# End of a fused attention and feed-forward kernel: last attention output kept in SBUF, last pair of token tiles taken one by one, the closing list chosen from many orders

## Chip, cores and metric

The kernel runs on one NeuronCore of a Trainium2 chip. The metric is the device time of one execution in microseconds (us), here the median of three runs. The engines are TensorE (PE in the profile, its weight loads PEld), VectorE (DVE), ScalarE (ACT), GpSimd (POOL) and SyncE (SP), which issues all DMAs of this kernel.

## Reference

```python
x = x + tanh(g_xattn) * attention(layernorm(x), ctx)      # 16 heads of 32, pad mask over x's rows
x = x + tanh(g_ffn) * ffn(layernorm(x))
# attention: q = x Wq^T, k and v from ctx Wkv^T, softmax(q k^T / sqrt(32)) v
# ffn:  h = bitlinear(x, w1, b1); h = gelu(h) (exact); bitlinear(h, w2, b2)
# bitlinear: rmsnorm, activations rounded to 127 steps of the row's maximum,
#            weights rounded to -1, 0, 1 times their mean size
```

x is 32 x 224 x 512, ctx 32 x 750 x 384, w1 goes from 512 to 2048 and w2 back. All inputs are float32.

## Kernel before

**Tiling.** Attention is cut into 128 steps (b, g): 32 batches times 4 groups of 4 heads. A step has six slots `k`: the maxima of the scores (`sm`, DVE's `mx`), the weights (`se` on PE, then Exp into `p` on ScalarE, sums `acc` on GpSimd) and, for the step before, the values (`po`) and their sums. VectorE transposes `po` into `oT` and takes the reciprocal `rd` of the sums (`sums`); `finish` multiplies the two into `yo` on GpSimd; `store` writes `yo` with four DMAs (one per head) to `o_d`, a scratch tensor in DRAM that holds the attention output token by token.

The feed-forward part works on 56 tiles of 128 tokens, taken in 28 pairs (`TG = 2`, `NF = 28`, numbered 0 to 27). `ffn_units(i)` gives the units of one pair. For both tiles together: `load` (x; and `og`, the attention output, out of `o_d`), `add`, `stats`, `rsqrt`, `norm`, `max`, `sa0` to `sa2` (scales of the rounding), `grid`, `bias`, `round`, `turn` (two transposing DMAs into `xT`). For each tile t: `b{t}0` to `b{t}3` (PE's `ph` from `xT` and w1; VectorE writes h out of it), `gelu`, `square`, `hm` (maxima), `sb0` to `sb2` (scales), `cgrid`, `cround`, `cturn` (a transposing DMA into `hT`), `c{t}0` and `c{t}1` (PE's `po` from `hT` and w2; VectorE adds it to x), `out` (store). In the records the h of pair 26 is called `wq_sb` and `wkv_sb`, and x and attention output of the last two pairs are both `xo`, after the buffers that they reuse.

**Order.** Every instruction is kept in program order on its engine by a helper (line 52 of the kernel before, so nearly every record has that line). In the loop, `Ffn.fill` starts feed-forward units slot by slot where there is room and `ready` says that what they need was started long enough ago. A Gelu in the loop loads its table and then, by a dummy Exp called `warm`, the table of Exp again.

After the loop, `Ffn.drain` writes out everything that is left, one unit after the other: the last attention step (`top`: the copy of the negative maxima `nT`; `w0` to `w2`: weights; `val`, `fin0`, `sto0`: values, division and store of the step before; `vlast`, `fin1`, `sto1`: of the last step) and the rest of pairs 25, 26 and 27. It is one greedy list: of the units that could begin soonest, by planned durations `TAKES_US` and free times of the engines, the one with the longest way to the end goes next. For a unit with two ways (VectorE or GpSimd, ScalarE or VectorE) the planner chooses the earlier end, with VectorE's time counted twice; `small[0]` then holds the engine for the unit. `behind` lists what a unit has to stand behind; the fetch of the last pair's attention output stands behind `sto1`:

```python
"fetch": [(NF, "sto1")],
...
f"b{t}0": [(pair, "turn")]
```

Of the kernel before, what the change touches and what calls it, by code (L numbers as in the profile page):

```python
# [19 lines left out]
EPS = 1e-5  # L20
# [4 lines left out]
def flamingo_gated_layer(  # L25
# [420 lines left out]
    def finish(b, g):  # L446
# [6 lines left out]
        yo_of[b, g] = yo  # L453

    def store(b, g):
        yo = yo_of.pop((b, g))
        for j in range(HG):
            cols = slice(g * P + j * DH, g * P + (j + 1) * DH)
            sp.dma_start(
                o_d[b * S : (b + 1) * S, cols].rearrange("(c r) d -> r c d", r=DH),  # L460
                yo[j * DH : (j + 1) * DH],
            )
# [72 lines left out]


    draining = []
    NTI = NT // P
    TG = 2
    NF = NTI // TG  # L540

    def quant_scales(s, r, amax, n, tag, unit):

        a = smf.tile([P, n], F32, tag=f"{tag}_am", name=f"{tag}_am")
        c = smf.tile([P, n], F32, tag=f"{tag}_c", name=f"{tag}_c")
        s[tag] = c, a
        if n == 1:  # L550
            small[0].tensor_scalar(a, amax, r, 1e-5, ALU.mult, ALU.max)
        else:
            small[0].tensor_tensor(a, r, amax, ALU.mult)
            small[0].tensor_scalar(a, a, 1e-5, None, ALU.max)
        yield
        dve.reciprocal(c, a)
        yield
        if n == 1:
            small[0].tensor_scalar(c, c, 127.0, r, ALU.mult, ALU.mult)
        else:  # L560
            small[0].tensor_scalar(c, c, 127.0, None, ALU.mult)
            small[0].tensor_tensor(c, c, r, ALU.mult)
        small[0].tensor_scalar(a, a, unit, None, ALU.mult)
# [7 lines left out]
    def ffn_units(i):  # L571
# [6 lines left out]
        def a_load():  # L578
# [11 lines left out]
            if i < NF - 1:  # L590
                a_fetch()

        def a_fetch():
            sp.dma_start(s["og"], o_d[rows, :].rearrange("(t p) d -> p t d", p=P))

# [19 lines left out]
        def a_norm():  # L615
            if i < NF - 2:
                s["xc"] = fp.tile([P, TG, D], F32, tag="xc", name=f"xc_{i}")
            else:
                both = vp.tile([P, NKC * D // 2], F32, tag="v", name=f"xc_{i}")
                s["xc"] = both[:, : TG * D].rearrange("p (t d) -> p t d", t=TG)  # L620
                s["xq"] = both[:, TG * D :].bitcast(BF16).rearrange("p (t d) -> p t d", t=TG)
            for t in range(TG):
                to, of, by = s["xc"][:, t, :], s["xg"][:, t, :], s["nm"][:, t : t + 1]
                if small[0] is dve:
                    dve.tensor_scalar(to, of, by, None, ALU.add)
                else:
                    act.activation(to, of, AF.Identity, bias=by)
# [36 lines left out]
        def b_matmul(t, f):  # L664
# [11 lines left out]
            for k in range(NDC):  # L676
# [4 lines left out]
            dve.scalar_tensor_tensor(  # L681
                s["h", t][:, cols], ph, s["qa"][1][:, t : t + 1], b1_sb[:, cols],
                ALU.mult, ALU.add,
# [63 lines left out]
        ]  # L747
        if i == NF - 1:
            first[1:] = [("fetch", 0, "load", 0, 0, 0, a_fetch), ("add", 0, "fetch", 0, 0, 0, a_add)]
        first += [  # L750
# [10 lines left out]
            ("turn", 0, "round", 0, 0, 0, a_turn),  # L761
        ]
        parts = [first]
        for t in range(TG):
            part = []
            for f in range(4):
                part.append((
                    f"b{t}{f}", 0 if f else 3, f"b{t}{f - 1}" if f else "turn", 0.9, 0, 0.75,
                    lambda t=t, f=f: b_matmul(t, f),
                ))  # L770
# [32 lines left out]
        "sb2": [[("DVE", 0.4)], [("POOL", 0.6)]], "cgrid": [[("DVE", 1.7)], [("POOL", 2.0)]],  # L803
        "cround": [[("ACT", 2.0)], [("DVE", 1.8)]], "cturn": [[("SP", 3.8)]],
        "c": [[("PE", 1.75), ("DVE", 0.5)]], "out": [[("SP", 2.0)]],
        "top": [[("PE", 0.3), ("ACT", 0.4)]],
        "w": [[("PE", 1.1), ("ACT", 1.7)]],
        "val": [[("PE", 2.9), ("DVE", 0.9)]], "vlast": [[("PE", 4.0), ("DVE", 0.9)]],
        "fin": [[("POOL", 0.6)]], "sto": [[("SP", 3.6)]],
    }  # L810

    QUEUE_US = {"sto": 1.9, "turn": 1.9, "cturn": 1.5, "load": 0.5, "fetch": 0.5, "out": 0.4}

# [3 lines left out]
        for name, after in {  # L817
            "w0": "top", "w1": "w0", "w2": "w1", "val": "", "fin0": "val", "sto0": "fin0",
            "vlast": "w2 val", "fin1": "vlast fin0", "sto1": "fin1 sto0",
        }.items()  # L820
    }

    class Ffn:
# [3 lines left out]
        def __init__(self):  # L827
            self.slot = 0
            self.parts = []
            self.next = 0  # L830
            self.at = {}

        def behind(self, pair, name):
# [3 lines left out]
                "load": [(pair - XG, f"out{TG - 1}"), (pair - 1, "add")],  # L837
                "fetch": [(NF, "sto1")],
                "norm": [(pair - 1, "round")],
# [5 lines left out]
            if name[-1].isdigit():  # L845
                t = int(name[len(name.rstrip("0123456789"))])
                (p1, t1), (ph, th) = (divmod(pair * TG + t - n, TG) for n in (1, HB))
                before = {
                    f"b{t}0": [(pair, "turn")]
                    + [(ph - (pair == NF - 1), f"cround{th}")] * (pair != NF - 2),  # L850
# [12 lines left out]
        def ready(self, pair, unit):  # L863
            name, lag, after = unit[:3]
            lag = lag if not draining else 0
            if after is not None:
# [43 lines left out]
        def drain(self, more):  # L910
# [3 lines left out]
            draining.append(True)  # L914
            free = {"PE": 0.0, "ACT": 0.0, "DVE": 4.3, "POOL": 5.0, "SP": 0.0}
            end = {}

            def takes(name):
                kind = name.rstrip("0123456789")
                return TAKES_US.get(kind) or TAKES_US[kind + name[-1]]  # L920

            self.parts.insert(0, [NF, more])
            while self.next < NF:
                self.parts += [[self.next, part] for part in ffn_units(self.next)]
                self.next += 1
            left = {}

            def rank(at):

                if at not in left:  # L930
                    left[at] = 0.0
                    left[at] = sum(us for _, us in takes(at[1])[0]) + max(
                        (rank(x) for x in behind if at in behind[x]), default=0.0
                    )
                return left[at]

            behind = {
                (pair, u[0]): [(pair, u[2] or "")] + self.behind(pair, u[0])
                for pair, units in self.parts for u in units
            }  # L940

            def course(at, way):

                t = max(
                    [end.get(x, 0.0) for x in behind[at]
                     if x[1].rstrip("0123456789") not in ORDER_ONLY or x[1][:-1] != at[1][:-1]],
                    default=0.0,
                )
                t = begin = max(t, free[way[0][0]])
                for engine, us in way:  # L950
                    t = max(t, free[engine]) + us
                return begin, t

            while self.parts:
                self.slot += 10
                found = []
                for part in self.parts:
                    for unit in part[1]:
                        if self.ready(part[0], unit):
                            at = part[0], unit[0]  # L960
                            way = min(
                                takes(unit[0]), key=lambda way: course(at, way)[1]
                                + 1.0 * sum(us for engine, us in way if engine == "DVE"),
                            )
                            found.append((course(at, way)[0], -rank(at), part, unit, way))
                soon = min(f[0] for f in found) + 2
                t, _, part, unit, way = min((f for f in found if f[0] <= soon), key=lambda f: f[1])
                part[1].remove(unit)
                self.at[part[0], unit[0]] = self.slot
                small[0] = {"DVE": dve, "POOL": gp}.get(way[-1][0], act)  # L970
                unit[6]()
                for engine, us in way:
                    t = max(t, free[engine])
                    free[engine] = t + (QUEUE_US[unit[0].rstrip("0123456789")] if engine == "SP" else us)
                    t += us
                end[part[0], unit[0]] = t
                self.parts = [p for p in self.parts if p[1]]
            return end

# [52 lines left out]
    for n in range(N - 1):  # L1032
# [56 lines left out]
        for k in range(6):  # L1089
# [13 lines left out]
            if wunits:  # L1103
                if k in (1, 3, 5):
                    wunits.pop(0)()
            else:
                some = ffn.fill(
                    (PE_ROOM[k % 2] - used, (1.1, 2.2)[k % 2], 1.7),
# [18 lines left out]
            for name, at, *do in (  # L1127
                ("val", last[0], values, sums), ("fin0", last[0], finish), ("sto0", last[0], store),
                ("vlast", last[1], values, sums), ("fin1", last[1], finish), ("sto1", last[1], store),
            )  # L1130
# [40 lines left out]
```

## Time and profile before

| | us |
|---|---|
| median of three runs | 2996.57 (2995.82, 2996.57, 2997.93) |
| profiled execution, its own time | 2990.66 |
| its span | 2988.9 |
| PE busy | 2891.5 (97%) |
| POOL busy | 2081.6 (70%) |
| DVE busy | 1725.5 (58%) |
| ACT busy | 1417.8 (47%) |
| last 99 us (from 2890): PE busy | 59.5 |

The profile is of one execution. Its records tell when an instruction started on its engine, how long it took, and what ended an idle time ahead of it. The clock of PE is granted by a throttle, and the windows of the profile give its mean in parts of full speed. The median of the runs is 5.91 us above the profiled execution.

### The profile page before, as it was taken

What the parts mean: (1) busy time and instruction counts of PE and PEld (TensorE: products, weight loads), DVE (VectorE), ACT (ScalarE), POOL (GpSimd) and SP (SyncE); (2) the same over time, 40 slices, a digit from 0 to 9 for tenths busy, and PEclk for the clock granted to TensorE, in tenths of its full rate; (3) what the DMA queues carried; (4) which work ended last, traced back from release to release, by engine and by line L of the source; (5) the groups of instructions that cost most, each with busy time, mean ns of one, the idle gap of its engine ahead of it and who ended that gap; (6) DMA issues with size and microseconds to landing.
All of it is one profiled execution on the core that took longest, in us unless ns stands there. A gap on an engine that the chain in (4) does not pass through costs nothing.

```text
span 2988.9 us, 62964 instructions
## 1 busy us (share of the span) xinstructions
PE 2891.5 (97%) x26814; PEld 1839.9 (62%) x26814; DVE 1725.5 (58%) x2588; ACT 1417.8 (47%) x1438; POOL 2081.6 (70%) x2727
## 2 busy tenths in 40 slices
PE   8999999999999999999999999999999999999976
PEld 5666566666666666666666666666666666666643
DVE  5576555655555565556555555654655655556545
ACT  2344454544545455445445454553543554545444
POOL 3566767767777777767667777767767777687674
PEclk9999999999999999999999999999999999999987
DMA  5433223123222212221222222223122222321213
GB/s 152 106 95 98 54 57 79 35 59 73 53 58 63 58 48 70 65 68 32 57 72 53 58 61 64 46 58 75 44 49 65 48 69 63 69 74 27 46 45 79
DMA packets 376697, 190.03 MB, mean 64 GB/s; under 512 B 283104, under 2 KB 340576, under 8 KB 376288
## 3 DMA queue, kind: packets, MB, share of 16 engines
q1 hardware_dynamic: 376416, 186.02, 25.8%
q8 instruction: 209, 3.42, 0.5%
q14 instruction: 72, 0.59, 0.1%
HBM read 119.86 MB, written 29.39 MB: 50 GB/s over the span
## 4 chain that ended last, share of the span: by engine, by line
PE 82%; ACT 10%; POOL 3%; DVE 3%; issue 1%; DMA 1%; POOLq 0%; ACTq 0%; SPq 0%; DVEq 0%
PE po L52 17%; PE pk L52 14%; PE se L52 14%; PE sm L52 12%; PE pv_None L52 8%; ACT p L52 7%; PE ph L52 6%; PE pv L52 6%; PE pq L52 3%; DVE mx L52 2%; ACT L52 2%; POOL acc L52 1%; ACT h L52 1%; PE pn L52 1%; POOL r_a L52 1%
## 5 line engine op out<-in xcount | busy, mean ns | idle before, releaser
L52 POOL TENSOR_TENSOR acc<-acc,p 125x896 f32<-125x896 f32 x510 | 1066.0, 2090 | 325.7 <-ACT p L52 304.2
L52 DVE TENSOR_REDUCE mx<-sm 112x4 f32<-112x2000 f32 (+1 forms) x384 | 861.0, 2242 | 664.5 <-PE sm L52 662.6
L52 ACT ACTIVATE p<-se 125x1792 f32<-125x1792 f32 x384 | 639.1, 1664 | 759.0 <-PE se L52 701.6
L52 PE MATMUL pk<-y,wkv_sb 128*128 128x375 f32 x1536 | 538.3, 486 | 2.0 <-DMA y<-in_ctxT 2.0
L52 PE MATMUL sm<-kT,qT 32*112 32x500 f32 (+1 forms) x4096 | 426.7, 508 | 31.6 <-ACT p L52 22.7
L52 POOL TENSOR_TENSOR acc<-p 125x896 f32<-125x896 f32 x128 | 268.3, 2096 | 244.4 <-ACT p L52 244.3
L52 PEld LDWEIGHTS pk<-y,wkv_sb 128*128 128x128 f32 x1536 | 277.8, 189 | 174.4 <-issue 34.5
L52 PE MATMUL se<-qT,kT 32*125 32x224 f32 x6144 | 359.5, 348 | 0.0
L52 PE MATMUL po<-p,v 125*32 125x224 f32 x6144 | 318.1, 355 | 0.0
L52 PE MATMUL pv<-wkv_sb,y 128*125 128x256 f32 x1248 | 311.0, 385 | 0.0
L52 PEld LDWEIGHTS se<-qT,kT 32*125 32x125 f32 x6144 | 295.5, 183 | 0.0
L52 PEld LDWEIGHTS sm<-kT,qT 32*112 32x112 f32 x4096 | 159.2, 170 | 190.1 <-ACT p L52 138.7
L52 PEld LDWEIGHTS po<-p,v 125*32 125x32 f32 x6144 | 186.9, 110 | 119.5 <-issue 44.0
L52 PEld LDWEIGHTS pv<-wkv_sb,y 128*125 128x125 f32 x1248 | 223.2, 188 | 52.3 <-issue 17.8
L52 ACT COPY kT<-pk 128x375 f32<-128x375 f32 x256 | 120.3, 470 | 278.8 <-PE pk L52 278.0
L52 PE MATMUL pv_None<-wkv_sb,y 128*125 128x256 f32 x1056 | 250.9, 387 | 0.0
L52 PEld LDWEIGHTS pv_None<-wkv_sb,y 128*125 128x125 f32 x1056 | 191.2, 187 | 89.0 <-issue 59.7
L52 PE MATMUL po<-w2q,hT 128*128 128x256 fp8e4 x1792 | 222.1, 280 | 24.4 <-DMA hT<-hq 24.4
L52 DVE SCALAR_TENSOR_TENSOR h<-ph,qa_am,b_sb 128x512 f32<-128x512 f32 x216 | 158.9, 745 | 139.0 <-PE ph L52 111.1
L52 PE MATMUL ph<-w1q,xT 128*128 128x512 fp8e4 x896 | 226.1, 384 | 4.8 <-DMA xT<-xc 4.8
L52 PE MATMUL pq<-xTb,wq_sb 128*128 128x224 f32 x1024 | 221.4, 359 | 0.4 <-DVE wq_sb L52 0.4
L52 PEld LDWEIGHTS <-hT 128*128 128x128 bf16 x1792 | 171.8, 100 | 76.6 <-issue 27.1
(131 smaller groups left out, 2863.1 us busy)
## 6 DMA issues: line engine op xcount, KB each, us to landing
y<-in_ctxT SPq DMA_DIRECT2D x90, 375.0 KB, 4.7
x<-in_x SPq DMA_DIRECT2D x32, 448.0 KB, 4.0
xTb<-in_xT SPq DMA_DIRECT2D x32, 448.0 KB, 3.7
o_d<-yo SPq DMA_DIRECT2D x512, 28.0 KB, 1.9
xg<-in_x SPq DMA_DIRECT2D x26, 512.0 KB, 3.8
og<-o_d SPq DMA_DIRECT2D x26, 512.0 KB, 4.4
out<-xg SPq DMA_DIRECT2D x52, 256.0 KB, 2.2
wa<-in_w1T SPq DMA_DIRECT2D x8, 512.0 KB, 5.6
```

Source lines behind the costliest of these rows:

```text
L52: return lambda *args, **kw: tc.keep_in_program_order(build(*args, **kw))
```

## The change

Four things are changed, all at the end of the program.

1. The output of the last attention step is not written to `o_d` and read back. `finish_last` divides it into an SBUF tile `last_o` (set to zero by GpSimd first), in pieces of 32 partitions that go straight to the rows where the last pair wants them: twelve instructions on VectorE (unit `fin1`) and four on ScalarE (`fin2`). The fetch of the last pair takes the other three head groups (128x2x384) and the 32 older rows of the last group, and stands behind `sto0`.
2. The last pair's units up to the transposition are done tile by tile (`ladd0`, `lstats0`, ... `lturn0`, and the same for tile 1); `b{t}0` stands behind its own `lturn{t}`.
3. `drain` tries 8300 orders, 300 from ranks with random additions and then variations of the best, by a model of the engines and queues (with a slower PE after a hole of over 2 us), and writes out the best. `QUEUE_US` and `TAKES_US` get entries for the new units, and `cturn` is planned with 4.2 instead of 3.8.
4. In the last step of the loop, from slot 3, the units `gelu`, `add`, `rsqrt`, `grid`, `bias`, `cgrid` and `sb` are not started (`closing`, `NOT_LAST`).

```diff
+    def finish_last(two):
+        b, g = steps[-1]
+        oT, rd = po_of[b, g]
+        if not last_o:
+            last_o.append(pp.tile([P, TG, P], F32, tag="p", name="last_o"))
+            gp.memset(last_o[0], 0.0)
+        first = b * S - (NF - 1) * TG * P
+        quads = {}
+        for c in range(S // DH):
+            quads.setdefault((first + c * DH) % P, []).append(c)
+        for at, cs in quads.items():
+            if (len(cs) > 1) != two:
+                continue
+            for j in range(HG):
+                rows = slice(j * DH, (j + 1) * DH)
+                cols = slice(j * DH, (j + 1) * DH)
+                to, c = last_o[0][at : at + DH, :, cols], cs[0]
+                if two:
+                    cc = slice(c, cs[1] + 1, P // DH)
+                    dve.tensor_tensor(
+                        to, oT[rows, 0, cc, :],
+                        rd[rows, cc].unsqueeze(2).to_broadcast([DH, TG, DH]), ALU.mult,
+                    )
+                else:
+                    act.activation(
+                        to[:, (first + c * DH) // P], oT[rows, 0, c, :], AF.Identity,
+                        scale=rd[rows, c : c + 1],
+                    )
...
         def a_fetch():
-            sp.dma_start(s["og"], o_d[rows, :].rearrange("(t p) d -> p t d", p=P))
+            of = o_d[rows, :].rearrange("(t p) d -> p t d", p=P)
+            if i < NF - 1:
+                sp.dma_start(s["og"], of)
+                return
+            sp.dma_start(s["og"][:, :, : D - P], of[:, :, : D - P])
+            sp.dma_start(s["og"][:old, 0, D - P :], of[:old, 0, D - P :])
+        def l_add(t):
+            cols = slice(D - P, D)
+            small[0].tensor_tensor(
+                s["xg"][:, t, cols], s["xg"][:, t, cols], last_o[0][:, t, :], ALU.add
+            )
...
+    NOT_LAST = "gelu", "add", "rsqrt", "grid", "bias", "cgrid", "sb"
...
-                "fetch": [(NF, "sto1")],
+                "fetch": [(NF, "sto0")],
...
-                    f"b{t}0": [(pair, "turn")]
+                    f"ladd{t}": [(NF, "fin1"), (NF, "fin2")],
+                    f"b{t}0": [(pair, f"lturn{t}" if pair == NF - 1 else "turn")]
...
+            if self.closing and name.rstrip("0123456789") in NOT_LAST:
+                return False
...
+            rng = random.Random(1)
+            every, best = sorted(todo), None
+            for n in range(8300):
+                if n < 300:
+                    like = {at: rank(at) + rng.uniform(0.0, 12.0) * (n > 2) for at in every}
+                    args = (0.4, 1.0, 2.0)[n % 3], rng.choice((0.3, 0.6, 1.0))
+                else:
+                    like, args = dict(best[2]), best[3]
+                    for at in rng.sample(every, rng.choice((1, 2, 4, 8))):
+                        like[at] += rng.uniform(-15.0, 15.0)
+                us, order = course(like, *args)
+                if best is None or us <= best[0]:
+                    best = us, order, like, args
...
+                ffn.closing = n == N - 2 and k > 2
...
-                ("vlast", last[1], values, sums), ("fin1", last[1], finish), ("sto1", last[1], store),
+                ("vlast", last[1], values, sums), ("fin1", (True,), finish_last),
+                ("fin2", (False,), finish_last),
```

## Prediction

> **What bounds the kernel now.** I read the page first, then the waits of the last 95 us, the timeline of the same stretch, and the windows with the granted clock. TensorE is busy for nearly the whole span, so only a stretch where it stands still can give time back.
>
> ```profile
> PE 2891.5 (97%) x26814; PEld 1839.9 (62%) x26814; DVE 1725.5 (58%) x2588; ACT 1417.8 (47%) x1438; POOL 2081.6 (70%) x2727
> ```
>
> The loop ends near 2889.7 and the span at 2988.9. In the waits of that end, PE stands 24.4 us for the transposed h, 4.8 for the transposed x, 4.9 behind a ScalarE copy:
>
> ```profile
> PE po L52 <- DMA hT<-hq: 24.4, 5, 13.5
> ...
> POOL xo L52 <- DMA xo<-o_d: 9.6, 1, 9.6
> ...
> PE se L52 <- ACT nT L52: 4.9, 1, 4.9
> PE ph L52 <- DMA xT<-xc: 4.8, 1, 4.8
> ```
>
> The timeline shows both places that the change touches. First, a Gelu with a table load on each side stands between the last Exp of the loop and the copy `nT` that the last attention step needs:
>
> ```profile
> 2888.03 1.66 ACT L52 ACTIVATE p<-se 125x1792 f32<-125x1792 f32 x1 [3.60 <-PE se L52]
> ...
> 2889.71 1.28 ACT L52 ACT_TABLE_LOAD   x1
> ...
> 2891.00 1.91 ACT L52 ACTIVATE h<-h 128x2048 f32<-128x2048 f32 x1
> 2892.93 1.28 ACT L52 ACT_TABLE_LOAD   x1
> ...
> 2894.33 0.33 ACT L52 COPY nT<-pn 128x224 bf16<-128x224 bf16 x1
> 2894.71 0.64 PE L52 MATMUL se<-nT,ones 3*125 3x448 bf16 x4 [4.88 <-ACT nT L52]
> ```
>
> Second, the last attention output goes to DRAM and back (start, duration; `yo` is held behind POOL's `xc` and `xo<-xo,b2g`), and the last pair's statistics wait for it:
>
> ```profile
> 2910.36 0.20 DVE L52 RECIPROCAL rd<-oT 128x7 f32<-128x7 f32 x1
> ...
> 2911.39 2.49 POOL L52 TENSOR_TENSOR xo<-xo,b2g 128x512 f32<-128x512 f32 x2
> ...
> 2913.84 0.57 POOL L52 TENSOR_TENSOR yo<-oT,rd 128x224 f32<-128x224 f32 x1
> ...
> 2915.24 1.99 SPq L52 DMA_DIRECT2D o_d<-yo  x4
> ...
> 2919.89 0.38 SPq L52 DMA_DIRECT2D xo<-o_d  x1
> ...
> 2923.99 2.35 POOL L52 TENSOR_TENSOR xo<-xo 128x1024 f32<-128x1024 f32 x1 [9.58 <-DMA xo<-o_d]
> ...
> 2927.25 0.68 DVE L52 BATCH_NORM_STATS2 st<-xo 128x6 f32<-128x512 f32 x1
> ```
>
> The clock makes standing still cost twice (columns: busy times by engine, clock, DMA):
>
> ```profile
> 2930.00:2940.00 10.00, 2.27 (x11) 1.60 (x12) 6.50 (x8) 4.52 (x6) 7.63 (x29) 0.50 0.28 54
> ```
>
> The clock is granted in windows of 3.413 us. In this trace every window in which PE was busy under 0.40 was followed by one at half clock (7 of 7), and 0.44 stayed at full; back to full came only behind a fully busy one. The end has 12 half-clock windows.
>
> **How I cost it.** Each engine runs its instructions in program order, and the changed program's order is known. I carried both orders forward from 2889.7 by one rule: an instruction starts when its engine is free and its inputs have landed, lasts as long as its row, and PE's clock follows the windows. The old order then lands its last store at 2987.92; the trace has 2987.84. Around the span lie 1.76 us (profiled execution 2990.66), and the median of 2996.57 is 5.91 above that execution, so I take differences and hang them on the median.
>
> **Part 1: no Gelu just ahead of the last step.** Two table loads (2 x 1.28), the Gelu (1.91), a dummy Exp (0.20) go from ScalarE ahead of `nT`: with `p` over at 2889.69, `nT` can start at 2889.88 when `pn` is done, and `se` at 2890.27, not 2894.71: -4.4. Its 20 matmuls then run at full clock (1.15 as in the next step, not 2.13) and the first sums no longer wait at half clock: the next `se` starts 2894.59 against 2900.55, -6.0. The Gelu returns after the last Exp (load 2900.75, Gelu 2901.94; one load is saved), where ScalarE has nothing else and its consumer, the first `hT` turn, is still issued at 2923.5 against 2933.40. Nothing waits for it sooner. This part alone, put into the old order, moves the last landing from 2988.7 to 2982.8 (means over the clock's positions, see below): **-5.9**.
>
> **Part 2: last output in SBUF.** Removed: `yo` (0.57), four stores (landed 4.45 after the first issue), the wait of the fetch for them. The fetch (128x2x384, then 32x128) now waits only for the step before and is asked for at 2906.6; taking 3.9 for the large part (the fetch of 1024 above landed after 3.96) and 1.7 for the small one (one of the stores), it has landed at 2912.2. Added: a POOL memset (0.31, the row for 112x256), queued behind the rsqrt chain of pair 25, so done at 2909.84; 12 DVE pieces of 32x2x32 and 4 ScalarE pieces of 32x32. No row has that form: the nearest are 0.16 (tensor_tensor 128x1), 0.19 (tensor_scalar 112x64) and 0.39 (128x224). I take 0.28, bounds 0.16 and 0.39: 3.4 us on DVE, ending near 2913. Queued behind them are the eight h-writes of pair 26, so PE's `ph` stops with its banks full at 2908; nothing else covers that, so each 0.1 us more per piece costs 1.2 at the end. POOL adds lie on the line through 1.27 (512 elements) and 2.36 (1024): 1.81 for 768, 0.46 for each of the three of 128, so they end at 2915.7. Statistics of tile 0 then start at 2919.8 (behind the h-writes), 7.5 earlier than 2927.25.
>
> **Part 3: tile by tile, and another list.** The quantising chain of pair 26 and its grid and bias (2 x 0.68, 2 x 1.25 on POOL, just ahead of `yo` before) go to DVE: 6 x 0.17, 2 x 0.48 (tensor_scalar 128x512), 2 x 0.7 (no row; 128x512 statistics 0.67, h-write 0.75) and a rounding of 0.8 (128x1024 0.74 to 1.09), in a hole while PE does the last scores. The first tile's xT turn is issued at 2928.1 and the second's at 2936.6, against 2938.72 for both. Each tile pays its own small chain of ten (about 0.27 each on POOL, 0.21 on DVE); the second runs beside PE's work on the first. The last Gelu starts 2945.5 (2954.12 before: -8.6). From it to the last `hT` issue it took 23.1 us, because POOL's chain for that tile began only at 2968.44; in the new order POOL reaches it at 2954.2 and the way is 17.2: -5.9. The last turn is issued at 2962.66 instead of 2977.21, **-14.5**; behind it lie the same 4.3 + 3.7 + 0.5 + 2.0 as now. Half-clock windows: 5 instead of 12. On SP an `out` store stands ahead of this turn and waits for DVE until 2962.07, 0.6 us before the turn is wanted: a late DVE there costs what exceeds it.
>
> **What is taken off.** That sum has the clock windows where the profile had them and pieces at 0.2. Nothing in the records ties the windows to the kernel's start, and the three times spread by 2.1 us, so I shift the windows through all positions: old order 2987.2 to 2990.4, mean 2988.7; new with pieces at 0.28, mean 2976.8: **-11.9** (at 0.2 -12.7, at 0.39 -10.5). With all new forms 0.75 to 1.9 times their rows and transposes up to 0.6 longer the gain has a median of 8.9 (6 to 13.5): an order searched for one set of durations loses by any other. Between 11.9 and 8.9 I take **-10.4**: 2986.2. The Trainium skill, "TensorE: Matmul & The Clock Gate", section "What's actually happening", calls the window free-running and 3413 ns long; the window length agrees with this trace's 3.413. By the profile's own position the sum would be 2996.6 - 14.5 = 2982.1, by a free position 2986.
>
> **Rivals.**
> (a) *Only part 1 pays.* The rest waits for something else: the list fits no real durations, SP's queue turns in the wrong order. For it: PE has a hole in the new order from 2918.6 to 2927.8 with nothing to fill it. Against: the last Gelu-to-turn way is shorter by POOL's order alone. -5.9: 2990.7.
> (b) *The pieces collide with POOL.* A POOL operation of 0.23 (`ve`) took 1.28 at 2929.34, exactly as long as the DVE grid that began 0.06 before. At 0.2 the pieces end 0.36 us before POOL's 1.81 add starts; above 0.23 they meet it, and DVE or POOL is 1.8 later: 2988.0. The Trainium skill, "SBUF — State Buffer", section "Who interferes with whom", says that a vector instruction with two SBUF inputs and a GpSimd one that reads SBUF shut each other out for a whole instruction; the `ve` row shows it for a one-input grid, none here for two inputs.
> (c) *Cheap pieces, lucky windows*, -14.5: 2982.
> (d) *Slower: expensive pieces.* Twelve short instructions that read 32 partitions and write other 32, all ahead of the h-writes PE waits for. At 12 us of end per us of piece, the gain of 12.7 is gone at 0.2 + 12.7/12 = 1.26 us each; at 1.8 each the time is 3003. Against it: no small DVE row exceeds 0.39. For it: no row has their partitions.
>
> **Numbers.** Forecast 0.62, (a) 0.15, (b) 0.10, (c) 0.08, (d) 0.05. What a measurement can tell from no change is 0.2%, 6.0 us: faster is below 2990.6. (a) lies on that border and is halved. Faster 0.62 + 0.07 + 0.10 + 0.08 = 0.87; same 0.08 + 0.01 = 0.09; slower 0.04. The range goes from (c), 2982.0, to (a), 2991.0.
>
> **What would show it.** In the changed profile: no table load between the loop's last Exp and `nT`, PE's 4.9 wait for `nT` gone; pieces near 0.28, h-writes right behind; statistics of the first tile some 7 us earlier; fewer windows at half clock; the last `hT` issued 10 to 15 us earlier. Wrong if pieces exceed 0.6, if the fetch lands after 2915, or if the last turn waits behind a store.

## Result and the profile after

| | kernel before | changed kernel |
|---|---|---|
| median of six runs, us | 2996.03 (2990.98 to 2997.93) | 2984.76 (2982.41 to 2988.29) |
| ratio to before | | 0.9967, 95% interval 0.9956 to 0.9978 |
| profiled execution / its span, us | 2990.66 / 2988.9 | 2985.39 / 2983.6 |

The change makes the kernel faster by 0.33% (0.22 to 0.44). The forecast was 2986.2 in a range of 2982.0 to 2991.0.

The two spans differ by 5.3 us only, because the two executions did not reach the end at the same time. The third Exp of the kernel shows it, in the timelines of before and after, far from anything that was changed:

```profile
41.12 1.66 ACT L52 ACTIVATE p<-se 125x1792 f32<-125x1792 f32 x1 [0.55 <-PE se L52]
```

```profile
44.28 1.66 ACT L53 ACTIVATE p<-se 125x1792 f32<-125x1792 f32 x1 [0.55 <-PE se L53]
```

The clock records of the second have two half-clock windows from 32.7 on and one at 476.4; those of the first have none before 2861. So from here on I use the **end stretch**: from the end of the loop's last Exp to the end of the span. It was 2988.9 - 2889.69 = 99.2 us before and is 2983.6 - 2894.32 = 89.3 now, 9.9 less. Times written "+x" count from that Exp's end.

PE's share is the same, its waits in the last 99 us are not (page, then waits of the changed kernel: total, times, longest):

```profile
PE 2892.7 (97%) x26814; PEld 1840.7 (62%) x26814; DVE 1737.2 (58%) x2616; ACT 1414.2 (47%) x1438; POOL 2084.4 (70%) x2723
```

```profile
PE po L53 <- DMA hT<-hq: 20.7, 4, 12.4
...
POOL xo L53 <- DMA xo<-o_d: 7.4, 1, 7.4
...
PE ph L53 <- DMA xT<-xc: 4.2, 3, 2.6
```

The wait of 4.9 for `nT` is gone; the wait of POOL for the fetch, which the SBUF tile was to shorten, is still 7.4, where it was 9.6. The timeline of the changed kernel, for the lines shown of before:

```profile
2892.66 1.66 ACT L53 ACTIVATE p<-se 125x1792 f32<-125x1792 f32 x1 [3.60 <-PE se L53]
...
2894.51 0.34 ACT L53 COPY nT<-pn 128x224 bf16<-128x224 bf16 x1 [0.18 <-PE pn L53]
...
2902.42 2.11 DVE L53 TENSOR_SCALAR qa_am<-qa_am,w 128x2 f32<-128x2 f32 x1
2902.43 4.42 POOL L53 TENSOR_TENSOR acc<-acc,p 125x896 f32<-125x896 f32 x2 [1.64 <-ACT p L53]
...
2904.44 2.69 DVE L53 TENSOR_SCALAR xc<-xc,qa_c 128x512 f32<-128x512 f32 x2
...
2909.37 2.50 SPq L53 DMA_TRANSPOSE xT<-xc  x2
...
2911.97 2.00 SPq L53 DMA_DIRECT2D o_d<-yo  x4
...
2914.66 2.75 DVE L53 TENSOR_TENSOR last_o<-oT,rd 32x64 f32<-32x64 f32 x12 [0.97 <-POOL last_o L53]
...
2917.00 3.63 SPq L53 DMA_DIRECT2D xo<-o_d  x2
...
2921.99 2.34 POOL L53 TENSOR_TENSOR xo<-xo 128x768 f32<-128x768 f32 x2 [7.36 <-DMA xo<-o_d]
...
2925.18 0.69 DVE L53 BATCH_NORM_STATS2 st<-xo 128x6 f32<-128x512 f32 x1 [1.19 <-POOL xo L53]
```

Three things are to be read here. No table load stands between the Exp and `nT`. A VectorE instruction on 128x2, 0.17 us by itself, took 2.11 beside GpSimd's `acc`, and two grids of 0.48 took 2.69. And the stores of the step before (`o_d<-yo`) stand on SP behind the xT transpositions of pair 26, which VectorE's late rounding released only at 2909.37; the fetch stands behind the stores.

### The profile page after: what moved, and what is told of

It reads as the page before. It is cut to its first block, busy times and chain, and to the rows that moved or that the text cites. A ratio compares the mean times of both kernels' runs of the same rounds, so it can differ in the third digit from the quotient of the medians.

```text
span 2983.6 us, 62984 instructions
## 1 busy us (share of the span) xinstructions
PE 2892.7 (97%) x26814; PEld 1840.7 (62%) x26814; DVE 1737.2 (58%) x2616; ACT 1414.2 (47%) x1438; POOL 2084.4 (70%) x2723
## 4 chain that ended last, share of the span: by engine, by line
PE 82%; ACT 10%; POOL 3%; DVE 2%; issue 1%; DMA 1%; POOLq 0%; SPq 0%; ACTq 0%; DVEq 0%
PE po L53 17%; PE pk L53 15%; PE se L53 14%; PE sm L53 13%; PE pv_None L53 8%; ACT p L53 7%; PE pv L53 6%; PE ph L53 6%; PE pq L53 3%; DVE mx L53 2%; ACT L53 2%; POOL acc L53 1%; ACT h L53 1%; PE pn L53 1%; POOL h L53 1%
## 5 line engine op out<-in xcount | busy, mean ns | idle before, releaser
L53 PE MATMUL sm<-kT,qT 32*112 32x500 f32 (+1 forms) x4096 | 426.9, 508 | 31.6 <-ACT p L53 22.7
L53 PEld LDWEIGHTS pv<-wkv_sb,y 128*125 128x125 f32 x1248 | 223.3, 188 | 52.3 <-issue 17.8
```

The source lines that it names most:

```text
L53: return lambda *args, **kw: tc.keep_in_program_order(build(*args, **kw))
```

## Experiments

All are edits of the changed kernel but the first, and each was timed beside the kernel before. The end stretch is that of one profile. In the prediction's model, other positions of the clock windows move the end of the old order by 3.2 us (2987.2 to 2990.4), so smaller differences of single end stretches decide little.

| kernel | median, us | kernel before, timed with it | ratio, 95% interval | end stretch |
|---|---|---|---|---|
| only_closing | 2988.43 | 2992.47 | 0.9982 (0.9973 to 0.9991) | 92.5 |
| no_closing | 2985.16 | 2992.47 | 0.9974 (0.9963 to 0.9985) | 91.3 |
| first_order | 3010.61 | 2992.47 | 1.0059 (1.0047 to 1.0072) | 119.2 |
| dram_last | 2978.02 | 2992.47 | 0.9946 (0.9933 to 0.9958) | 84.4 |
| after_again | 2982.32 | 2994.64 | 0.9961 (0.9948 to 0.9973) | 89.3 |
| dram_same_list | 2983.38 | 2994.64 | 0.9962 (0.9950 to 0.9975) | 89.5 |
| pair_together | 2980.92 | 2994.64 | 0.9960 (0.9947 to 0.9974) | 87.3 |
| search_closing_only | 2985.84 | 2994.64 | 0.9970 (0.9959 to 0.9980) | 91.3 |
| dram_seed3 | 2987.20 | 2993.81 | 0.9976 (0.9967 to 0.9985) | 93.8 |
| dram_seed7 | 2978.95 | 2993.81 | 0.9947 (0.9934 to 0.9961) | 85.5 |
| sbuf_dram_list | 2985.12 | 2993.81 | 0.9970 (0.9959 to 0.9981) | 90.6 |
| sto_first | 2980.11 | 2993.81 | 0.9951 (0.9938 to 0.9963) | 85.5 |

**only_closing**: the kernel before with the fourth part alone.

```diff
+            if self.closing and name.rstrip("0123456789") in NOT_LAST:
+                return False
...
+            ffn.closing = n == N - 2 and k > 2
```

> The kernel before with the fourth part alone: gelu, add, rsqrt, grid, bias, cgrid and sb are not started in the last step of the loop, everything else (greedy list, last output through DRAM, last pair together) as before. Forecast's theory: this part alone is worth 5.9 us, so about 2990 against 2996, ScalarE's nT right behind the last Exp and the wait of 4.9 us for it gone from PE. Rival 1: the Gelu is only moved and the list waits for it later, 0 to 2 us, 2994 to 2996. Rival 2: nearly all of the change's gain is this part, 2985 to 2987.

0.18% faster (0.09 to 0.27, that is 2.7 to 8.1 us); the end stretch is 6.7 shorter. The mechanism is as told: `nT` follows the Exp.

```profile
2892.52 1.66 ACT L52 ACTIVATE p<-se 125x1792 f32<-125x1792 f32 x1 [3.60 <-PE se L52]
...
2894.36 0.35 ACT L52 COPY nT<-pn 128x224 bf16<-128x224 bf16 x1 [0.18 <-PE pn L52]
```

**no_closing**: `ffn.closing = False` in the changed kernel.

> The changed kernel with the fourth part taken out (closing always False), so that the Gelu with its two table loads stands ahead of the last nT again; the search finds a list of its own. Forecast's theory: loses 5.9 of the 11 us, about 2990.5. Rival (the parts overlap: the search hides the Gelu): within 2 us of the changed kernel, 2985 to 2987.

0.26% faster than before and, by the differences of the medians (7.3 against 11.3 and 12.3), 4 to 5 us less than the changed kernel, nearer to the forecast's theory; by the ratios it is 2 to 4, and the intervals overlap. End stretches: closing alone saves 6.7, everything but closing 7.9, both together 9.9 and not 14.6. So the gains do not add up here. Whether they overlap in themselves is not shown, since no_closing has a list of its own, and the seeds below move a list by 8 to 9 us.

**first_order**: the search cut to its first candidate.

```diff
-            for n in range(8300):
+            for n in range(1):
```

> The changed kernel with the search cut to the first candidate (the greedy list by plain ranks); last output in SBUF, tile by tile, no Gelu in the last step all kept. Theory A (the search carries the parts): carried forward by the rows this list ends 12 to 18 us after the list before, so 3008 to 3014. Rival B (the parts pay with any sensible list, the search adds one or two us): 2986 to 2988.

18 us slower than before, as theory A had it: all three other parts are in this kernel. But it is not the old list with these parts in it: the first candidate chooses among units that begin within 0.4 us of the soonest, the kernel before within 2, and it can weigh VectorE's time differently. So the run shows that the parts do not make up for a poor list, and not what they are worth under the old rule. Its list leaves PE waiting for xT and GpSimd for VectorE's `qb_c` (waits of this kernel):

```profile
PE ph L53 <- DMA xT<-xc: 29.2, 3, 23.2
...
POOL h L53 <- DVE qb_c L53: 24.1, 2, 16.9
```

This kernel also shows the collision of rival (b). GpSimd's add of 128x768 starts at 2924.44, while VectorE does the twelve pieces; one of them took 1.88 us, where the median is 0.22 (all instructions on `last_o`, shortest, median and longest in ns):

```profile
L53 DVE TENSOR_TENSOR last_o<-oT,rd x12: 215/216/1878, 2922.2 to 2926.3; 32x64 f32<-32x64 f32 x12
```

The rival had put 1.8 us on it. In the changed kernel the add starts only after the pieces, and the longest of them took 0.22.

**dram_last**: the first part undone, a list of its own.

```diff
-                ("vlast", last[1], values, sums), ("fin1", (True,), finish_last),
-                ("fin2", (False,), finish_last),
+                ("vlast", last[1], values, sums), ("fin1", last[1], finish), ("sto1", last[1], store),
...
-                "fetch": [(NF, "sto0")],
+                "fetch": [(NF, "sto1")],
```

> The changed kernel with the first part undone: the last output goes by yo, four stores and the fetch of 128x2x512 as before; tile by tile, search (a list of its own) and no Gelu in the last step are kept. Theory A, the forecast's: the SBUF tile is worth about half of the remaining 5 us and more, so 2987 to 2990. Rival B: statistics of the last pair are held by PE's and DVE's work on pair 26 as much as by the round trip, and a searched list hides the trip as well: 2982 to 2985, no slower than the changed kernel.

Rival B: 14.5 us under the kernel before, the lowest of all here. The part that was to save a round trip is not needed for the gain. One place where dram_last is ahead is PE's `ph` of pair 26, in the timelines of the changed kernel and of dram_last:

```profile
2918.25 3.61 PE L53 MATMUL ph<-w1q,xT 128*128 128x512 fp8e4 x16 [2.35 <-DVE wq_sb L53]
```

```profile
2909.90 7.08 PE L53 MATMUL ph<-w1q,xT 128*128 128x512 fp8e4 x32 [1.68 <-DMA xT<-xc]
```

In the changed kernel PE stands for the h-writes, which are queued behind the twelve pieces, and is done at +27.5; with no pieces it goes through at once, to +25.0. The add and the statistics of dram_last come no later for the round trip: its stores are issued at +18.0, its fetch at +22.7, the same as in the changed kernel.

**after_again, dram_same_list**: the changed kernel once more, and the changed kernel's own list with the round trip in place of the tile.

```diff
-                ("vlast", last[1], values, sums), ("fin1", (True,), finish_last),
-                ("fin2", (False,), finish_last),
+                ("vlast", last[1], values, sums), ("fin1", last[1], finish, store),
+                ("fin2", (False,), lambda two: None),
```

> The changed kernel itself once more, so that its runs stand beside those of this call on one chip. From the runs so far: 9 to 11 us below the kernel before. The stretch behind the loop's last Exp took 89.3 us in its profile (99.2 before); with other positions of the clock's windows 85 to 90 is expected of it.

> The changed kernel's own list, unit for unit, with the last output by yo (GpSimd, at the place of the twelve pieces), four stores and one fetch of 128x2x512, in place of last_o, the split fetch and the two small adds. It takes the SBUF tile away and leaves the order. Theory A (the tile saves the round trip, as forecast: statistics of the first tile about 4 us earlier than the rest of the list allows without it): 3 to 5 us slower than the changed kernel. Theory B (the h-writes of pair 26 hold the statistics back as long as the round trip does, and without twelve pieces on VectorE they come earlier): within 1.5 us of the changed kernel, the wait of the add for the fetch 3 to 5 us longer, but the h-writes 2 to 3 us earlier.

The ratios are 0.9961 and 0.9962, the end stretches 89.3 and 89.5: theory B. In this list the tile is worth nothing that these runs could tell. The timeline of dram_same_list tells why (its Exp ends at 2892.12):

```profile
2911.40 0.74 DVE L53 SCALAR_TENSOR_TENSOR wq_sb<-ph,qa_am,b_sb 128x512 f32<-128x512 f32 x1
...
2914.55 0.56 POOL L53 TENSOR_TENSOR yo<-oT,rd 128x224 f32<-128x224 f32 x1 [2.49 <-DMA o_d<-yo]
...
2918.30 0.38 SPq L53 DMA_DIRECT2D xo<-o_d  x1
2922.31 2.34 POOL L53 TENSOR_TENSOR xo<-xo 128x1024 f32<-128x1024 f32 x1 [7.20 <-DMA xo<-o_d]
2924.68 0.69 DVE L53 BATCH_NORM_STATS2 st<-xo 128x6 f32<-128x512 f32 x1 [5.56 <-POOL xo L53]
```

The h-writes begin at +19.3 (+23.1 in the changed kernel, behind the pieces), 3.8 earlier. The fetch is asked for at +26.2 instead of +22.7, the add starts at +30.2 instead of +27.7, but it is one add: statistics start at +32.6, only 1.7 later than the +30.9 of the changed kernel. That delay did not reach the end.

**pair_together**: last_o kept, the last pair through its units with both tiles at once, a list of its own.

> The changed kernel with the second part undone: last_o kept, but the last pair goes through statistics, scales, grid, rounding and transposition with both tiles at once; search (a list of its own) and no Gelu in the last step kept. Theory A (PE gets the first tile's matmuls 8 us earlier, which fills its hole): 2 to 5 us slower than the changed kernel. Theory B (the hole ends with the h of pair 25 all the same, and the list adapts): within 2 us.

0.9960: no slower. Theory B. Doing the last pair tile by tile is not needed either, if the list may change; with the order left as it is, it was not taken out.

**search_closing_only**: both of these parts undone, a list of its own.

> Search and no Gelu in the last step alone: last output by DRAM and last pair with both tiles at once, as before, a list of its own. Theory A (the first two parts pay 5 us together): 5 us slower than the changed kernel. Theory B (with the search they pay nothing by themselves): as the changed kernel. Carried forward with the rows and with VectorE and GpSimd shutting each other out, its list ends 5 us later than that of the changed kernel and 8 later than that of dram_last, 7.6 before the kernel before: a list found by a planner with round durations can be 5 us better or worse on the chip, so its time alone does not settle which part did it.

0.9970, end stretch 91.3: by the medians 3.5 us slower than the changed kernel beside it, with intervals that overlap. As its expectation says, this number alone cannot tell parts from lists.

**dram_seed3, dram_seed7**: dram_last with another seed.

```diff
-            rng = random.Random(1)
+            rng = random.Random(3)
```

> dram_last (last output by DRAM, tile by tile, search, no Gelu in the last step) with another seed of the search, random.Random(3) for random.Random(1): the same instructions, another list that the planner holds to be as good. Theory A (the parts set the time): as dram_last, about 14.5 us under the kernel before. Theory B (which list the planner lands on sets it, its durations being round and VectorE and GpSimd shutting each other out not being in them): carried forward with both, this list ends 8.8 us later than dram_last's, so only 5 to 7 us under the kernel before.

> The same with random.Random(7). Theory A: as dram_last. Theory B: carried forward, the list ends 1.6 us earlier than dram_last's and moves least with the positions of the clock's windows (1 us), so 15 to 17 us under the kernel before: a candidate for the best kernel.

Theory B. Three lists for the same units give 0.9946, 0.9976 and 0.9947; the first two intervals do not meet. The seed alone moves the time by 8 to 9 us (end stretches 84.4, 93.8, 85.5), more than any part of the change but the search itself. The lists differ in more than order: where a unit has two ways, the planner also chooses its engine, and the pages count 2613, 2601 and 2625 instructions on VectorE and 2709, 2722 and 2699 on GpSimd.

**sbuf_dram_list**: dram_last's list with the tile.

```diff
-                ("vlast", last[1], values, sums), ("fin1", last[1], finish), ("sto1", last[1], store),
+                ("vlast", last[1], values, sums), ("fin1", (True,), finish_last),
+                ("sto1", (False,), finish_last),
```

> dram_last's list, unit for unit, with the last output in the SBUF tile (twelve pieces on VectorE and four on ScalarE at the places of yo and its stores, the split fetch right behind the stores of the step before, the three small adds behind the large one). Theory A (the tile saves the round trip): 2 to 5 us faster than dram_last. Theory B (the pieces stand ahead of the h-writes that PE waits for and the trip was hidden): slower than dram_last; carried forward 7 us, so 7 to 8 under the kernel before.

0.9970 against 0.9946, intervals apart, end stretches 90.6 and 84.4: slower by about 6 us, as theory B had it, but not for its reason. The fetch, which I had put right behind the stores, stands ahead of pair 26's xT transpositions on SP. The rounding that these need was over at 2908.17; the timeline of sbuf_dram_list (its Exp ends at 2892.71) has them at 2912.33, that of dram_last (2892.02) at 2907.43:

```profile
2907.04 1.13 ACT L53 ACTIVATE xc<-xc,magic 128x1024 bf16<-128x1024 f32 x1
...
2908.62 3.62 SPq L53 DMA_DIRECT2D xo<-o_d  x2
...
2912.33 2.50 SPq L53 DMA_TRANSPOSE xT<-xc  x2
```

```profile
2907.43 2.51 SPq L53 DMA_TRANSPOSE xT<-xc  x2
```

That is +19.6 against +15.4, and PE's work on pair 26 waits as long. The pieces were over at 2912.88, and the first h-write began at 2916.78, after a wait for PE: they held nothing back there. So the transpositions' place in SP's queue went with most of the 6 us; what the tile alone does in this list the run does not tell.

**sto_first**: the stores of the step before go ahead of the xT transpositions of pair 26.

```diff
+            move((NF, "fin0"), (NF - 2, "turn"), behind=False)
+            move((NF, "sto0"), (NF, "fin0"))
```

> The changed kernel's list with one move: division and stores of the last step but one (fin0, sto0) ahead of the xT transpositions of pair 26, so that SP no longer holds these stores, and the last pair's fetch behind them, until VectorE has rounded. Theory: the fetch is issued 2 to 3 us earlier behind the loop's last Exp and the add's wait of 7.4 us for it shrinks by as much; the end gains 1 to 1.5 us only, since the h-writes of pair 26 end 0.7 us after the add could. Rival (the fetch alone holds the statistics): the end gains 3 us or more.

The timeline (its Exp ends at 2892.76):

```profile
2906.01 1.77 SPq L53 DMA_DIRECT2D o_d<-yo  x4
...
2907.89 2.51 SPq L53 DMA_TRANSPOSE xT<-xc  x2
...
2910.58 3.62 SPq L53 DMA_DIRECT2D xo<-o_d  x2
...
2915.71 2.34 POOL L53 TENSOR_TENSOR xo<-xo 128x768 f32<-128x768 f32 x2 [2.75 <-DMA xo<-o_d]
...
2922.23 0.68 DVE L53 BATCH_NORM_STATS2 st<-xo 128x6 f32<-128x512 f32 x1
```

The fetch is asked for at +17.8 instead of +22.7 and the wait for it falls from 7.4 to 2.75, more than expected; statistics start at +29.5, 1.4 earlier, now right behind VectorE's h-writes and a row maximum, with no wait for the add. The medians put it 1.4 to 2.4 us ahead of the changed kernel, within the intervals, nearer to the theory; the end stretch is 3.8 shorter, as the rival had it. The two do not decide between them. The place on SP's queue was the reason for the late fetch; how far it also moves the end is not shown.

## Why the prediction was right, and where it was not

The total was right: -10.4 forecast, -11.3 by the medians, -9.9 by the ratio and by the end stretches. It was so in part by luck. The steps of the sum came to 14.5, and the trace lost 1.7 up to the last Gelu, 1.4 from there to the last turn and 1.5 behind it. What the forecast took off for other clock positions and for longer instructions, 4.1, was about as much as that, but of these causes it had only the clock's in view, the 1.5 at the end. Step by step, against the kernel before:

- **No Gelu ahead of the last step.** `nT` 4.45 earlier (-4.4 forecast), the second `se` at +5.0 instead of +10.9 (-5.9; -6.0 forecast). Worth 5.9 alone; measured 2.7 to 8.1.
- **Pieces.** 2.75 us for twelve, 0.23 each; 0.28 taken. The four on ScalarE took 1.31 together. The rival of expensive pieces is out.
- **The fetch.** This step failed. It was to be asked for at 2906.6, +16.9, and was at +22.7. The sum had put the quantising chain of pair 26 into a hole of VectorE at the length of its rows. But GpSimd's `acc` was running there: the chain's last 128x2 instruction and the grids lost 1.9 and 1.7 us to it, the transposition and the stores queued behind it went out late. That is 3.6 of the 5.8; the prediction has too few times in between to place the rest. The fetch landed at +27.5, past the 2915 (+25.3) that the prediction had named as a sign of being wrong. The prediction had the mechanism, in rival (b), at the wrong place: it priced a collision at the pieces, where the add started only after them. The Trainium skill's "SBUF — State Buffer", section "Who interferes with whom", lets a tensor_scalar in a two-port mode and a GpSimd operation shut each other out for a whole instruction. The trace agrees: 2902.42 + 2.11 is 2904.53, where the first of the two `acc` additions of 2.1 ended. Cover hid nearly all of it: statistics at +30.9, where +30.1 was forecast and +37.6 was before.
- **Tile by tile.** First xT turn at +40.1 (+38.4 forecast, +49.0 before); last Gelu at +57.5 (+55.8 forecast, +64.4 before). As told, 1.7 late all along.
- **From the last Gelu to the last turn.** 18.6 us (17.2 forecast, 23.1 before). Of the 1.4 that is too much, 1.1 was again a collision, GpSimd's `qb_am` of 1.39 for 0.31 beside VectorE's grid at 2960.46. The last turn came at +76.1, 11.4 earlier than before (14.5 forecast for this position of the clock and pieces of 0.2).
- **Clock.** 7 half-clock windows in the end stretch instead of 12; 5 forecast. One fell on the last matmuls: 5.33 us instead of 3.67. Averaging over positions, rather than taking the profile's own, gave the better number. The rule that the prediction read off the clock (under 0.40 busy, then half clock; 0.44 stayed at full) does not hold throughout: cutting the changed trace at the changes of its clock, the window from 2899.85 on had PE busy 0.46 and was followed by half clock, the one from 2920.33 on had 0.45 and was not; and a window of 0.93 was enough to bring full clock back. The rule would have left the window from 2903.27 on at full clock.

What the prediction did not see is **which part earned it**. It wrote the saved round trip and the earlier first tile as the causes of what closing did not explain. The runs point to the list: the round trip put back into the same list costs nothing that could be measured (dram_same_list), put back with a list of its own it gives the lowest time (dram_last), the two tiles together are as fast (pair_together), and the parts with the first candidate for a list are 18 us slower than before (first_order). Neither the search alone nor the three other parts under the old list's rule were run, so the list's share by itself is not shown. Carrying the list forward instruction by instruction takes the order into account; reading the sum as prices of parts was the error.

dram_last is 14.5 us faster than the kernel before. Against the changed kernel its end stretch is 4.9 shorter and its median lies 2 to 3 us further below the kernel before, but the two were not timed together and their intervals just overlap. With seed 7 it is as fast. That the better of the lists was found by its seed means that another planner or a longer search may find more; this was not tried.

## What to carry to other kernels

When the end of a kernel is a list of dependent steps over five engines, cost a change on the list that it produces and not by the work that it removes: three lists for the same units differed here by 8 us, and a removed DRAM round trip in the same order by nothing that could be measured. A fetch put ahead of two transpositions on SP's queue went with some 6 us. Test a part by taking it out and leaving the order as it is, and again with an order of its own; and before trusting one list of a randomised search, run several. A step put into a hole of VectorE can take far longer than its row if GpSimd works at that moment.

## What was not expected of the hardware

- A VectorE tensor_scalar on 128x2 elements took 2.11 us (0.17 alone) beside a GpSimd addition, while the chain on 128x1 elements in the kernel before ran at its usual 0.14 to 0.27 beside a GpSimd addition (2925.01 to 2926.34). Small size did not protect the one; the other, with a single element per partition, was not held up. No run varies the size alone.
- Clock windows at the start of the program differ by run: two half-clock windows at 32.7 moved everything behind by 3.2 us in one profiled execution, and none came in the other. Single executions of this kernel are therefore compared from a common instruction on.
- The second of the two fetches, which writes other rows and columns of the same tile, was issued only when the first had landed: the chain of the changed kernel has 3.30 us for the first and 1.53 for the second, one after the other. The prediction had added them so, with 3.9 and 1.7; it does not say that SP's queue is held meanwhile, for 3.6 us (one fetch: 0.38).
